# A two-layer attention and convolution kernel: the first part in two passes in written order, and the last part paced with seven image-0 units and a one-image unit at the end

## The chip, the cores and the metric

The kernel runs on one core of one Trainium2 chip. The metric is the device time in microseconds. The times of the kernel before are the median of 3 runs, with the lowest and highest beside it. A profile is one execution of its own; all times within it count from its first instruction. PE is TensorE's matmul, PEld its weight load, DVE VectorE, ACT ScalarE, POOL GpSimd and SP SyncE, which here only issues DMAs.

## The reference

Input x is (2, 256, 64, 64) in fp32: two images of 256 channels and 4096 positions. Two layers follow each other, all in fp32.

```python
# layer 0: attention over all 4096 positions, 8 heads of 32 channels
m = resize(mask, (B, 1, 64, 64), 'bilinear')
q = conv1x1(x, Wq, bq) / sqrt(32); k = conv1x1(x, Wk, bk); v = conv1x1(x, Wv, bv)
fuse = softmax(q k^T) v
x = conv1x1(concat[x, fuse], Wf, bf) * m + x * (1 - m)
# layer 1: channel gate, attention in windows of 8x8, a spatial gate
x = x * sigmoid(relu(x ca_w1 + ca_b1) ca_w2 + ca_b2)
x = x + window_attention(x; qkv_w, out_w)          # 4 heads of 64
x = channel_shuffle(x, groups=4)
y = relu(bn1(conv7x7(x, sa_w1, groups=64)))
y = bn2(conv7x7(y, sa_w2, groups=64))
return x * sigmoid(y)
```

## The kernel before

An image is cut into 8 chunks of 512 positions (CH, NCHUNK). There are three parts.

*First part (L147 to L463).* The small inputs are prepared (mask resized, L147 to L180; batch norms folded into the rows of the 7x7 convolutions, L301 to L400; `w_s`, the DRAM copy of the convolutions' band matrices, filled with zeros at L389). In L204 to L265 each of the 16 chunks of x is loaded and multiplied: q and k (L219) into PSUM pairs of two banks, then v (L244). DVE adds the bias to q and k (L230), ACT squares them with the bias (L231), a matmul with `headsum` adds the squares over a head's 32 channels (L254) and DVE takes their maximum (L265). q, k and v go to DRAM in `q_s`, `k_s` and `v_s` by SP's queue. At the end the largest |q| times the largest |k| decides `flag` (L278), whether exp is safe without subtracting a row maximum; every engine reads it (L1147) and enters arm "a" (safe) or "b". In these inputs it is arm "a". The order of the instructions in this part is left to the framework's scheduler; from the arm on it is the written order (`tc.manual_schedule()`).

*Middle (L1090 to L1118).* One slot is an image, a query chunk, a group of 4 heads and 128 keys: 1024 slots. In each, PE makes the scores of four heads (L580), ACT their exp (L590), PE the products with v (L609), and DVE sums exp in `suma` (L611). Keys and values come in pieces of four slots on SP's queue (L507, L509), two pieces ahead. When a chunk's 64 slots are over, denominators and their reciprocal follow by `at(8..12)` a few slots later, and `stage(b, c)` is queued at 13: a generator that does the rest of the chunk (fuse matmul hy at L677, channel gate, window attention, output projection op at L898, sum into `xo` at L909, which goes to DRAM in `x_s`), one step every fourth slot. `bands()` writes the rows of the convolutions into `w_s` on POOL's queue, one DMA every sixth slot.

*Last part (L1120 on).* The convolutions work in 16 units of 4 channel groups (NU, UG): `conv1` (c1, L987), relu, `conv2` (c2, L1011), tanh (L1021) and scaling (L1027) on ACT, product with x on DVE (L1033), and stores, half on SP and half on POOL (L1039). The generator `convolve()` goes through a list of items (unit, images): units 0 to 8 (EARLY = 9) of image 0, units 0 to 8 of image 1, then units 9 to 15 of both images at once. Items of image 0 can run before the last chunk of image 1 is ready and are put between the steps of its stage:

```python
while later or stages:
    now[0] += 2
    run_later(); run_stages()
    if later or stages:
        next(conv)
staged.append(True)
for _ in conv: pass
```

Each `next(conv)` gives one c1, or one c2, or, from one yield to the next, a gate with its stores and the following c1. Within the generator c1 of item k+1 stands ahead of c2 of item k. Once `staged` is set, items that need image 1 load their x from `x_s` (`xla`). The weights of eight units are held in the buffers of exp (`load_w`, L959); unit u+8 is loaded after the image-1 gate of unit u.

Of the kernel before, what the change touches and what calls it, by code (L numbers as in the profile page):

```python
# [19 lines left out]
P = 128  # L20
KC = C // P
# [10 lines left out]
EARLY = 1 + EB  # L32
# [22 lines left out]
def conv_seq_kernel(ctx: ExitStack, tc: tile.TileContext, a, out):  # L55
# [50 lines left out]
    def load(name, shape, src, eng, pool=const):  # L106
        t = pool.tile(shape, F32, name=name)
        eng.dma_start(t, src)
        return t

# [29 lines left out]

    h2 = H // 2
    mhs = []
    mk = ctx.enter_context(tc.tile_pool(name="mk", bufs=2))
    for b in range(B):

        m3 = mk.tile([h2, 3, h2 + 2], F32, tag="m3", name=f"m3_{b}")
        for n in range(3):
            lo, hi = max(0, n - 1), min(h2, h2 + n - 1)  # L150
            at0 = lo - n + 1
            nc.gpsimd.dma_start(
                m3[at0 : at0 + hi - lo, n, 1 : h2 + 1], a["mask"][b][lo:hi, :]
            )
        nc.gpsimd.dma_start(m3[0:1, 0, 1 : h2 + 1], a["mask"][b][0:1, :])
        nc.gpsimd.dma_start(m3[h2 - 1 : h2, 2, 1 : h2 + 1], a["mask"][b][h2 - 1 : h2, :])
        nc.vector.tensor_copy(m3[:, :, 0:1], m3[:, :, 1:2])
        nc.vector.tensor_copy(m3[:, :, h2 + 1 : h2 + 2], m3[:, :, h2 : h2 + 1])
        mid = mk.tile([h2, h2 + 2], F32, tag="mid", name=f"mid_{b}")
        nc.vector.tensor_scalar_mul(mid, m3[:, 1], 0.75)  # L160
        mv = mk.tile([h2, 2, h2 + 2], F32, tag="mv", name=f"mv_{b}")
        mh = mk.tile([h2, 2, h2, 2], F32, tag="mh", name=f"mh_{b}")
        for o in range(2):
            nc.vector.scalar_tensor_tensor(
                mv[:, o], m3[:, 2 * o], 0.25, mid, ALU.mult, ALU.add
            )
        m75 = mk.tile([h2, 2, h2], F32, tag="m75", name=f"m75_{b}")
        nc.vector.tensor_scalar_mul(m75, mv[:, :, 1 : h2 + 1], 0.75)
        for o in range(2):
            nc.vector.scalar_tensor_tensor(  # L170
                mh[:, :, :, o], mv[:, :, 2 * o : 2 * o + h2], 0.25, m75, ALU.mult, ALU.add
            )
        mhs.append(mh)
    for b, mh in enumerate(mhs):
        for c in range(NCHUNK):
            dst = mask_s[b, c].rearrange("(w r o x) -> o r w x", w=NW, r=4, o=2)
            for o in range(2):
                nc.gpsimd.dma_start(
                    dst[o],
                    mh[4 * c : 4 * c + 4, o].rearrange("p (w x) t -> p w (x t)", w=NW),  # L180
                )


    nm = const.tile([P, B * NCHUNK], F32, name="nm")
    flag = const.tile([1, 1], I32, name="flag")
    with (
        tc.tile_pool(name="w0", bufs=1) as w0,
        tc.tile_pool(name="x0", bufs=3) as x0,
        tc.tile_pool(name="st0", bufs=2) as st0,
    ):  # L190
        def weight(n):
            return load(n, [P, KC, C], a[n].rearrange("(k p) o -> p k o", p=P), nc.scalar, w0)

        wq, wk, wv = weight("WqT"), weight("WkT"), weight("WvT")
        bias = {}
        for n in ("bq", "bk"):
            t = w0.tile([P, KC], F32, name=n)
            for g in range(KC):
                for j in range(HG):
                    h = HG * g + j  # L200
                    nc.scalar.dma_start(
                        t[32 * j : 32 * j + 32, g : g + 1], a[n][h % 2, :, h // 2 : h // 2 + 1]
                    )
            bias[n] = t  # L204

        for b in range(B):
            src = a["x"][b].rearrange("(k p) h w -> p k (h w)", p=P)
            for c in range(NCHUNK):
                x = x0.tile([P, KC, CH], F32, tag="x", name=f"x0_{b}_{c}")
                nc.sync.dma_start(x, src[:, :, c * CH : (c + 1) * CH])  # L210
                sqs = []
                for n, w in (("q", wq), ("k", wk)):
                    s = psum2(f"{n}0_{b}_{c}")
                    for g in range(KC):
                        for kc in range(KC):
                            rhs = x[:, kc, :]
                            if n == "q":
                                rhs = rhs.rearrange("p (r w c) -> p w r c", r=WS, w=NW)
                            nc.tensor.matmul(  # L219
                                s[:, g, :],  # L220
                                w[:, kc, g * P : (g + 1) * P],
                                rhs,
                                start=(kc == 0),
                                stop=(kc == KC - 1),
                            )
                    t = st0.tile([P, KC, CH], F32, tag=n, name=f"{n}st_{b}_{c}")
                    sq = st0.tile([P, KC, CH], F32, tag="sq", name=f"{n}sq_{b}_{c}", bufs=4)
                    bt = bias["b" + n]
                    for g in range(KC):
                        nc.vector.tensor_scalar_add(t[:, g, :], s[:, g, :], bt[:, g : g + 1])  # L230
                        nc.scalar.activation(  # L231
                            sq[:, g, :], s[:, g, :], AF.Square, bias=bt[:, g : g + 1]
                        )
                    sqs += [sq[:, g, :] for g in range(KC)]
                    if n == "q":
                        nc.sync.dma_start(q_s[b, c], t.rearrange("p g n -> p (g n)"))
                    else:
                        for g in range(KC):
                            nc.sync.dma_start(k_s[b, g, c], t[:, g, :])
                s = psum2(f"v0_{b}_{c}")  # L240
                sv = s.rearrange("p a (t o) -> p (a t) o", t=2)
                for m in range(4):
                    for kc in range(KC):
                        nc.tensor.matmul(  # L244
                            sv[:, m, :],
                            x[:, kc, m * P : (m + 1) * P],
                            wv[:, kc, :],
                            start=(kc == 0),
                            stop=(kc == KC - 1),
                        )  # L250

                norms = psum1(f"nrm_{b}_{c}")
                for i, sq in enumerate(sqs):
                    nc.tensor.matmul(  # L254
                        norms[32 * i : 32 * i + 32, :], headsum, sq, start=True, stop=True
                    )
                v = st0.tile([P, KC, 4, P], F32, tag="v", name=f"vst_{b}_{c}")
# [45 lines left out]
    def batch_norm(name, t):  # L303
# [9 lines left out]
        return sc, sh  # L313

    cw = ExitStack()
# [897 lines left out]
```

## Time and profile before

| what | value |
|---|---|
| median of 3 runs | 3078.66 us (3075.16 to 3081.13) |
| the profiled execution: its own time | 3070.01 us |
| its span, first to last instruction | 3068.2 us |
| PE busy | 2988.2 us, 97% |
| DVE busy | 2516.5 us, 82% |
| ACT busy | 2450.6 us, 80% |
| POOL busy | 344.7 us, 11% |
| first scores of the middle start at | 219.07 us |
| last product of the middle ends at | 2821.82 us |
| fuse matmul (hy) of the last chunk starts at | 2846.85 us |
| last PE instruction ends at | 3048.9 us |

The shares are averages over three parts with different limits: a part is to be read from its own timeline. Idle time of an engine counts only where another waits for it. In a timeline each line is a run of like instructions: start, length, engine, line, operation, and in brackets the idle time of the engine before it and what ended it.

### The profile page before, as it was taken

The numbers are of one execution on the slowest core, as the hardware profiler recorded it, in microseconds if no ns is written. First come the engines' busy times: TensorE is split into PE (matmuls) and PEld (weight loads), VectorE is DVE, ScalarE is ACT, GpSimd is POOL, SyncE is SP. The second block draws the span as 40 slices with busy tenths as digits, with TensorE's granted clock in tenths as the row PEclk, the third lists the DMA queues.
The fourth block names the chain that finished last, engine by engine and source line by source line (L and its number), as shares of the span: only waits on it lengthen the run. The fifth ranks groups of instructions, "written<-read, shape, count | busy, mean of one in ns | idle before, by whom it ended". The sixth has DMA issues, their size and how long they took to land.

```text
span 3068.2 us, 61291 instructions
## 1 busy us (share of the span) xinstructions
PE 2988.2 (97%) x25338; PEld 1015.0 (33%) x25338; DVE 2516.5 (82%) x1398; ACT 2450.6 (80%) x4122; POOL 344.7 (11%) x591
## 2 busy tenths in 40 slices
PE   8989989999999999999999999999999999999897
PEld 4442222232222222222232222323232223224675
DVE  3229989999999999998999999999999998988211
ACT  2239879898989898998989898989898988987423
POOL 7110000001010101010101001010101010000346
PEclk9989999999999999999999999999999999999998
DMA  6953112314141413242322214132413242314264
GB/s 197 356 162 76 59 50 64 67 63 72 59 81 60 75 64 69 66 75 68 66 66 61 66 59 73 59 74 61 78 60 68 70 71 66 109 57 134 61 203 97
DMA packets 160352, 264.20 MB, mean 86 GB/s; under 512 B 43944, under 2 KB 62620, under 8 KB 160064
## 3 DMA queue, kind: packets, MB, share of 16 engines
q1 hardware_dynamic: 133664, 221.72, 24.4%
q0 software_dynamic: 22432, 35.91, 8.4%
q8 instruction: 201, 3.29, 0.4%
q10 hardware_dynamic: 3968, 2.57, 0.3%
q14 instruction: 87, 0.71, 0.1%
HBM read 197.89 MB, written 65.21 MB: 86 GB/s over the span
## 4 chain that ended last, share of the span: by engine, by line
PE 70%; DVE 16%; issue 2%; DMA 2%; ACT 2%; POOL 1%; SPq 0%; DVEq 0%; ACTq 0%; POOLq 0%
PE sa L580 28%; PE ava L609 26%; DVE suma L611 15%; PE qka L748 4%; PE hya L677 4%; PE vwa L834 2%; PE c2a L1011 1%; POOL out_dram L1039 1%; PE c1a L987 1%; ACT ea L590 1%; PE opa L898 1%; DMA out_dram<-za 1%; PE sca L782 1%; PE rda L647 1%; PE pta L857 1%
## 5 line engine op out<-in xcount | busy, mean ns | idle before, releaser
L611 DVE TENSOR_TENSOR suma<-suma,ea 128x2048 f32<-128x2048 f32 x960 | 2198.7, 2290 | 86.0 <-ACT ea L590 1.8
L590 ACT ACTIVATE ea<-sa 128x512 f32<-128x512 f32 (+1 forms) x3072 | 2044.2, 745 | 85.0 <-PE sa L580 36.9
L580 PE MATMUL sa<-qa,ka 32*128 32x512 f32 x8192 | 1189.9, 641 | 8.2 <-DMA ka<-ks 8.0
L609 PE MATMUL ava<-ea,va 128*32 128x512 f32 x8192 | 1092.3, 605 | 0.3 <-ACT fa L619 0.3
L580 PEld LDWEIGHTS sa<-qa,ka 32*128 32x128 f32 x8192 | 333.1, 183 | 762.8 <-ACT ea L590 688.6
L609 PEld LDWEIGHTS ava<-ea,va 128*32 128x32 f32 x8192 | 161.6, 108 | 780.6 <-issue 754.3
L924 POOL DMA_DIRECT2D xs<-xo x94 | 65.9, 708 | 2353.5 <-DVE xo L909 2353.4
L1039 POOL DMA_DIRECT2D out_dram<-za x192 | 108.0, 571 | 128.1 <-DVE za L1033 92.4
L748 PE MATMUL qka<-ua,qkv_w 128*128 128x512 f32 x256 | 118.4, 605 | 0.7 <-DVE ua L738 0.7
L1033 DVE TENSOR_TENSOR za<-za,xla 128x768 f32<-128x768 f32 (+1 forms) x16 | 20.9, 1309 | 101.4 <-ACT za L1027 65.0
L1011 PE MATMUL c2a<-yca,wa 32*128 32x192 f32 (+1 forms) x1400 | 100.0, 427 | 0.3 <-ACT za L1021 0.3
L685 ACT ACTIVATE ta<-hya,bf 128x512 f32<-128x512 f32 x32 | 20.2, 684 | 96.9 <-PE hya L677 96.9
L1011 PEld LDWEIGHTS c2a<-yca,wa 32*128 32x128 f32 x1400 | 91.8, 316 | 10.9 <-issue 9.7
L689 DVE TENSOR_TENSOR ta<-ta,mca 128x512 f32<-128x512 f32 x32 | 22.0, 689 | 88.0 <-ACT ta L685 88.0
L1021 ACT ACTIVATE za<-c2a 128x384 f32<-128x384 f32 (+1 forms) x50 | 26.3, 578 | 79.7 <-DMA out_dram<-za 47.9
L803 ACT ACTIVATE ewa<-ewa,mxwa 128x64 f32<-128x64 f32 x256 | 85.5, 362 | 0.0
L611 DVE TENSOR_TENSOR suma<-ea,ea 128x2048 f32<-128x2048 f32 x32 | 73.1, 2286 | 15.0 <-DMA va<-vs 15.0
L231 ACT ACTIVATE qsq<-q,bq 128x512 f32<-128x512 f32 x32 | 22.0, 687 | 74.1 <-DVE qst L230 72.6
L430 POOL DMA_DIRECT2D ws<-r2s x112 | 69.5, 623 | 68.5 <-DMA xs<-xo 33.2
L761 ACT ACTIVATE qka<-qka,qkv_b 128x512 f32<-128x512 f32 x64 | 40.7, 694 | 44.2 <-PE qka L748 44.2
L987 PE MATMUL c1a<-xla,wa 128*32 128x192 f32 (+1 forms) x896 | 58.7, 413 | 14.2 <-DMA xla<-xs 14.2
L230 DVE TENSOR_SCALAR qst<-q,bq 128x512 f32<-128x512 f32 x32 | 24.0, 751 | 59.1 <-PE q L219 41.2
(139 smaller groups left out, 1674.7 us busy)
## 6 DMA issues: line engine op xcount, KB each, us to landing
ka<-ks SPq DMA_DIRECT2D x256, 256.0 KB
va<-vs SPq DMA_DIRECT2D x256, 256.0 KB
ws<-zero POOLq DMA_DIRECT2D x16, 896.0 KB, 17.1
wa<-ws SPq DMA_DIRECT2D x16, 896.0 KB
xs<-xo POOLq DMA_DIRECT2D x78, 140.0 KB, 7.2
xla<-xs SPq DMA_DIRECT2D x23, 420.0 KB
x<-in_x_dram SPq DMA_DIRECT2D x16, 512.0 KB
ks<-kst SPq DMA_DIRECT2D x32, 256.0 KB
```

The source lines that it names most:

```text
L430: nc.gpsimd.dma_start(band2[:, at0 : at0 + step * (n - 1) + 1 : step, :], spread(r2_s[k : k + 1, :, i], n),)
L580: nc.tensor.matmul(heads[j], k[r, cols], q[r, g, :], start=True, stop=not shifted)
L590: nc.scalar.activation(e[:, h, :], tile, AF.Exp, scale=SCALE0)
L609: nc.tensor.matmul(av[r, :], v[:, m % PB, r], e[:, j, :], start=start, stop=stop)
L611: nc.vector.tensor_add(total, first[0] if m == 1 else total, e)
L677: nc.tensor.matmul(s[:, oc, :], wf[:, kc, oc * P : (oc + 1) * P], xw[kc] if kc < KC else f[:, kc - KC, :], start=(kc == 0), stop=(kc == 2 ...
L748: nc.tensor.matmul(s[:, j, :], wqkv[:, kc, o : o + P], u[:, kc, :], start=(kc == 0), stop=(kc == KC - 1),)
L803: nc.scalar.activation(e[:, n, :], e[:, n, :], AF.Exp, bias=mx[:, n : n + 1], accum_out=rs[:, n : n + 1],)
L924: eng.dma_start(x_s[b, n, p + r0 : p + r1].rearrange("r g w -> g r w"), xo[64 * h : 64 * h + 64, oc, r0 - WS * c : r1 - WS * c, :],)
L987: nc.tensor.matmul(s[32 * j : 32 * j + 32, 0 : n * W], w[:, j, d, :], xs[k][:, 0:n, j, d : d + W], start=(d == 0), stop=(d == KS - 1),)
L1011: nc.tensor.matmul(tiles[j // 2][:, j % 2, 0 : n * W], w[r, d], y[r, 0:n, d : d + W], start=(d == 0), stop=(d == KS - 1),)
L1039: eng.dma_start(dst[b, i, r0:r1, UG * u : UG * u + UG, :], z[p + r0 : p + r1, :, nb * m + n, :],)
```

## The change

First part. It now runs under `manual_schedule`, in the order of the text, in two passes. Pass 1 does q and k of all 16 chunks; pass 2 does v. All 16 chunks of x stay in SBUF between them. The squares of a chunk are gathered in one tile, DVE takes the maximum over each four neighbouring positions (a new reduce, 128x2048 to 128x512), and the norm matmuls and their reduce run on a quarter of the columns, one chunk later. The flag is computed while pass 2 runs. The v stores move from SP's queue to POOL's. The preparations become a generator, `prepare`, of which one step follows each chunk, and the loads of the weights of the later parts (`pending`) are issued on ACT, four after a chunk. In the arm a one-element exp (`warm`) is put ahead of the first slot.

Stage. The fuse matmul does the x half for both outputs first, then the half with f.

Last part. EARLY is 7: units 0 to 6 of image 0, units 1 to 6 of image 1, units 7 to 15 of both, and at the end unit 0 of image 1 alone. Ahead of the denominators stand two c1; `later` is stepped by one, with one conv step in it; in the stage a conv step follows only the steps that yield True (hy, u, first and second projection, pt, o). x of the image-1 items is requested at the first resumption after `staged`. Stores alternate between POOL and SP; those of the last item between ACT and SP.

```diff
-EARLY = 1 + EB
+DN = 8
+EARLY = 7
...
+    def prepare(mk, cwp):
...
+        for u in range(NU):
+            nc.gpsimd.dma_start(w_s[u], zero)
+            if u % 4 == 3:
+                yield
...
+        def norms(i, tops):
+            s = psum1(f"nrm_{i}")
+            for n in range(2 * KC):
+                s_ = s[32 * n : 32 * n + 32, 0 : CH // 4]
+                nc.tensor.matmul(s_, headsum, tops[:, n, :], start=True, stop=True)
+            nc.vector.tensor_reduce(nm[:, i : i + 1], s[:, 0 : CH // 4], AX.X, ALU.max)
...
+        for i, (b, c) in enumerate(chunks):
+            load_chunk()
...
+            nc.vector.tensor_reduce(
+                tops, sq.rearrange("p g (n f) -> p g n f", f=4), AX.X, ALU.max
             )
+            if i:
+                norms(i - 1, last)
+            last = tops
+            for t, src in pending[4 * i : 4 * i + 4]:
+                nc.scalar.dma_start(t, src)
+            next(prepared, None)
...
+        for i, (b, c) in enumerate(chunks):
+            s = psum2(f"v0_{b}_{c}")
...
+            for g in range(KC):
+                nc.gpsimd.dma_start(v_s[b, g, c], v[:, g].rearrange("p m d -> p (m d)"))
+            if i == 0:
+                norms(len(chunks) - 1, last)
+                nc.vector.tensor_reduce(top, nm, AX.X, ALU.max)
+            elif i == 1:
...
+                nc.vector.tensor_scalar(flag, prod, (SAFE / SCALE0) ** 2, None, ALU.is_le)
...
-            for oc in range(KC):
-                for kc in range(2 * KC):
...
+            for half in range(2):
+                for oc in range(KC):
+                    for kc in range(KC * half, KC * half + KC):
...
-            yield
+            yield True
...
-        items = [(u, (b,)) for b in range(B) for u in range(EARLY)]
-        items += [(u, tuple(range(B))) for u in range(EARLY, NU)]
+        items = [(u, (0,)) for u in range(EARLY)] + [(u, (1,)) for u in range(1, EARLY)]
+        items += [(u, (0, 1)) for u in range(EARLY, NU)] + [(0, (1,))]
...
+                last = k == len(items) - 1
+                engines = (nc.scalar, nc.sync) if last else (nc.gpsimd, nc.sync)
...
-                            eng = nc.sync if i >= 2 else nc.gpsimd
-                            eng.dma_start(
+                            stores += 1
+                            engines[stores % len(engines)].dma_start(
...
                 conv1(k + 1)
                 yield
+                more()
                 z = conv2(k)
                 yield
+                more()
                 gate(k, z)
...
+        nc.scalar.activation(warm, ones[0:1, 0:1], AF.Exp)
...
-        while later or stages:
-            now[0] += 2
+
+        next(conv)
+        while later:
+            now[0] += 1
             run_later()
-            run_stages()
-            if later or stages:
+            if now[0] == len(slots) + DN:
+                next(conv)
+        while stages:
+            if run_stages():
                 next(conv)
```

The steps of `prepare` between its yields are, in order: loads of mask, bn1 and raw1 (ahead of chunk 0); loads of bj and bn2; loads of raw2, the memsets of m1, m2 and `zero`, and the zero rows of `x_s`; mask arithmetic and its 16 stores, one step per image; the scalings of qkv_b, out_b, ca_b2 and WfT minus the identity; the first add of the three batch norms and their square roots on ACT; the rest of the batch norms; m1, `cbias1` and the store of `r1_s`; m2 in two steps; the store of `r2_s` and the zero writes to `w_s`, four to a step. Their operations are those of the kernel before.

## The prediction

> **What bounds the kernel now.** I read the busy shares by slice, then the busy time by stage, then the timelines of the two ends. The rows by stage (start:end, length, busy time of PE, PEld, DVE, ACT, POOL with counts, clock, DMA share, GB/s):
>
> ```profile
> 0.00:219.00 219.00, 197.60 (x650) 101.77 (x650) 68.79 (x141) 62.98 (x85) 78.66 (x156) 0.97 0.69 242
> 219.00:2822.00 2603.00, 2582.44 (x21557) 749.96 (x21561) 2402.83 (x1215) 2305.93 (x3884) 155.84 (x241) 1.00 0.29 69
> ...
> 2907.00:2920.00 13.00, 0.18 (x4) 0.18 (x8) 1.29 (x2) 1.06 (x2) 1.51 (x3) 0.65 0.45 108
> ```
>
> The middle (2603 us) is PE at 99%, and the change leaves its instructions alone but for an order inside L677. What can move are the first 219 us and the last 246.
>
> First part, TensorE timeline (start, length, instruction, idle before it):
>
> ```profile
> 197.06 3.70 PE L219 MATMUL q<-x,WqT 128*128 128x512 f32 x8
> 200.60 3.60 PE L219 MATMUL k<-x,WkT 128*128 128x512 f32 x8
> 204.03 3.62 PE L244 MATMUL v<-WvT,x 128*128 128x256 f32 x16
> ...
> 208.03 0.60 PE L254 MATMUL nrm<-qsq,headsum 128*32 128x512 f32 x2
> ...
> 219.07 3.79 PE L580 MATMUL sa<-qa,ka 32*128 32x512 f32 x14 [7.96 <-DMA ka<-ks]
> ```
>
> A chunk is 3.54 for q, 3.54 for k, 3.55 for v, about 0.9 for norms: 11.5 us. Sixteen are 184 of the 204 us that the stage takes. Then the flag is made, the branch taken, keys fetched; the first exp starts at 222.47, after a table load of 1.28 us at 221.18. VectorE in a backlogged chunk shows the second limit:
>
> ```profile
> 52.97 0.74 DVE L230 TENSOR_SCALAR qst<-q,bq 128x512 f32<-128x512 f32 x1
> ...
> 54.53 0.75 DVE L230 TENSOR_SCALAR qst<-q,bq 128x512 f32<-128x512 f32 x1
> 55.20 0.74 DVE L230 TENSOR_SCALAR kst<-k,bk 128x512 f32<-128x512 f32 x1
> 56.75 0.75 DVE L230 TENSOR_SCALAR kst<-k,bk 128x512 f32<-128x512 f32 x1 [0.81 <-ACT ksq L231]
> ```
>
> DVE and ACT take turns on one PSUM tile; the last square of this chunk ends at 58.23, 5.26 us after the first start.
>
> Last part:
>
> ```profile
> 2903.05 3.70 PE L898 MATMUL opa<-ota,out_w 128*128 128x512 f32 x8 [1.33 <-ACT ota L887]
> ...
> 2919.82 4.71 PE L987 MATMUL c1a<-xla,wa 128*32 128x192 f32 x56 [13.07 <-DMA xla<-xs]
> 2924.47 3.58 PE L1011 MATMUL c2a<-yca,wa 32*128 32x192 f32 x56
> 2927.98 2.53 PE L987 MATMUL c1a<-xla,wa 128*32 128x192 f32 x56
> ...
> 2985.22 4.80 PE L987 MATMUL c1a<-xla,wa 128*32 128x384 f32 x56
> 2989.95 4.96 PE L1011 MATMUL c2a<-yca,wa 32*128 32x384 f32 x56
> ```
>
> and, in POOL's timeline,
>
> ```profile
> 3048.23 13.45 POOL L1039 DMA_DIRECT2D out_dram<-za x24 [2.87 <-DVE za L1033]
> ```
>
> PE waits 13.07 us for the last chunk to pass through DRAM, its next c1 takes 4.71 instead of 2.53, and after PE ends (3048.9) POOL issues stores for 13 us more. A one-image unit costs 5.97 (2.46 + 3.51), a two-image unit 9.63.
>
> **The Trainium skill.** "PSUM — Partial Sum Buffer", section on bank collisions: ACT and DVE may not read one bank's quadrant at once; the trace agrees with such turns (0.81 and 0.82 us waits). "VectorE: DVE Perf Modes", perf-mode tier table: a reduce has only the one-element rate (0.96 GHz clock there); the trace has 0.69 us for 512 elements (L265, L794), which fits 512/0.96 + 156 ns. "TensorE: Matmul & The Clock Gate", on HAM oscillation: PE drops to half clock after an idle window of about 3.4 us; the c1 of 4.71 agrees. "DMA: Bandwidth & Descriptors", queues and rings: an engine takes its queues in turn; here the burst of zero writes (72 to 126 us, over 400 GB/s) left SP's stores late.
>
> **First part, step by step.**
> *Start.* ACT's bias loads and table load hold its first square to 15.41, as now. In the written order the chain is: q square to 16.1, second q bias and square to 17.64, k to 19.85, then the new reduce to 22.2.
> *New reduce.* 128x2048, by the 512-element row's rate 2048/0.96 + 156 = 2.29 us (a 2048-wide add takes 2.29 too). Not in the trace with groups of four: lower bound 2.2, upper bound twice that; I take 2.29.
> *A chunk of pass 1.* DVE: 5.26 to the last square, 2.25 reduce, 0.22 norm reduce (128 columns): 7.73 us. PE: 7.07 + 0.25 (norms on a quarter of the columns) = 7.3. So DVE with its turns becomes the bound. Fifteen more chunks: 116, to 138.2.
> *Preparation by hand.* Its DVE work now sits in that chain: masks 2.6, scalings 0.9, batch norms 4.0, band rows 2.7 (rows of 17 to 25, 33, 50 to 54 and 63 to 72 us) = 10.2, and about 1.3 for the square-root table load: pass 1 ends at 149.7. Its loads are issued on POOL from 5 us and are down before their chunk; ACT's weight loads, four of about 0.45 us a chunk, lie in the 2.5 us in which DVE reduces. If a load is late, DVE stops and with it the pass.
> *Pass 2.* v of chunk 0 is done before the last norms, which PE awaits until about 150.0; then 15 x 3.55 = 53.2, 0.4 for the flag's row, 1.05 for bvf: 204.7. ACT's copies (1.01 each) fit. The v stores leave SP for POOL, behind 16 zero writes: these become issuable when the band rows are done (about 104) and need 54 us, so v stores land from about 160. Two v buffers and three PSUM pairs hold five chunks, to 164, so PE should not stop. Bounds of the burst: 0 and, as now, 8 us; I take 2. POOL's own issue is 32 x 0.55 = 18 us, against 57 us.
> *Branch.* The flag is ready early, SP can load queries, keys and values during pass 2, and the Exp table load (warm) is behind the last v copy. Each engine reads the flag in 0.49 us and POOL issued 0.6 later, so about 1.1, all of it now on the path: scores at 207.8, first exp at 208.9 against 222.47. That is **-13.6**; if the branch or reused memory holds the loads back to the end of pass 2, 6 us less (the present 212.6 to 219). I book **-13**.
>
> **Middle.** L677 has the same 16 matmuls, x first; ACT waited for the whole pair anyway (2853.96 after 2853.93). Zero; with f ready no less than nothing either.
>
> **Last part.**
> *Before hy.* Last products at 2821.82. Fillers ahead of hy fall from four c1 and three c2 to two and one: 2 x 2.46 + 2 x 3.51 = 11.95 earlier, hy ends at about 2842. f is ready by about 2838 (denominators 3.0 with their gap of 1.07, reciprocal, c2 and its tanh, two copies, one multiply), under the x half of hy.
> *The stage.* Five c1 and five c2 become three and three: 11.9 less. Steps now uncovered: about 0.5 before ca1, 0.5 before ca2 and 2.4 before pt (last exps, v copy, normalise), of which 1.8 to 2.5 was idle before: net -11. The stage's last matmul ends at 2883.8 instead of 2906.7.
> *The wait.* It stays 13.1 us, but c1, c2, c1, c2 of image 0 now stand ahead of the first waiting c1: 11.94. About 1.2 idle, and no slow clock.
> *Units.* 18 single and 7 double become 14 and 9: -4 x 5.97 + 2 x 9.63 = -4.6 us of PE.
> *The end.* The last unit is single and stores on ACT and SP; SP is busy with 12 stores of the double before it until 6.5 us after PE's end, then 6 more at 0.42: 9.0 us of issue after PE against 12.8 now, -3.8.
> Sum: idle -11.9, slow clock -2.2, units -4.6, end -3.8, about 0.5 bubbles: **-22**. Against it: six units in a row fetch weights (917 KB), a double's x and write 256 KB in 5.97 us, 340 GB/s; now three do, and PE lost 1.14 us at 2976. Bounds 0 and 6 more; I take 1: **-21**.
>
> Together -34 on the profiled execution: span 3068.2 to 3034, its own time 3070 to 3036. That execution lies 8.6 under the median; carried to the median 3078.66, **3044.7**.
>
> **Rivals.**
> *Burst and turns eat the first part.* The zero writes meet stores of a faster pass (1.5 MB in 7.73 us is 194 GB/s, in before 2 MB in 11.5) and v stores queue behind them: first part gains 0 to 4, the last part stays: about 3056. For it: DMA share 1.0 from 80 to 130. Against: the x loads end early in the burst, and the stores alone need 129.
> *PE stays the bound.* If DVE and ACT need no turns, or nothing of the burst shows: pass 1 at 7.3, another 6 to 8 us: about 3037.
> *Last part bound by DMA and SP.* The six dense units run at the transfer rate and gates queue behind xla loads: -10 there, 3055.
> *Slower: the reduce with groups of four.* On the path 16 times. At 4.4 us the gain of 34 is used up; at 6.6, three times my value, 16 x 4.3 = +69, net +35: 3114. For it: no such row in the trace. Against: 64-element and whole-row groups cost the same 0.69.
> *The change doesn't do what it says:* the norm bound becomes coarser (it takes the maximum over four tokens), and could send the program into the arm with row maxima. Worked out from the inputs, the product is 16,718 against a limit of 115,200: excluded.
>
> **How the numbers follow.** Forecast 0.58; first part lost 0.13; PE-bound 0.10; last part short 0.08; slower 0.09, and 0.02 where a partly slow reduce cancels the rest. Below 3031 I leave 0.06, above 3067 the 0.11 of the last two: range 3031 to 3067. Within 0.2% (6 us, what this kernel's runs can tell from no change) 0.02; slower 0.09; faster 0.89.
>
> **What would show it.** Right: reduce rows of about 2.3 us, chunks of 7.7 in pass 1, scores near 208 with no wait for ka, under 3 us idle before the first image 1 c1, last POOL store about 8 us after PE. Wrong: a reduce over 4 us; DVE waiting for a load in pass 1; PE idle over 3 us at the v stores or the branch; waits for xla among the units of image 1.

## The result, and the profile after

| | before | after |
|---|---|---|
| median of 5 runs | 3078.79 us (3075.16 to 3081.46) | 3062.25 us (3056.05 to 3067.97) |
| profiled execution: own time, span | 3070.01, 3068.2 | 3056.05, 3054.1 |

The ratio is 0.9955, with a 95% interval of 0.994 to 0.997: faster by 16.5 us in the medians and by 14 in the two profiled executions. The forecast was 3044.7, or 34 us. The direction was right and the time lies in the range, but the forecast gain is twice the measured one.

First the busy time by stage of the kernel after, with the columns of the table shown of before (start:end, length, busy time of PE, PEld, DVE, ACT and POOL, clock, DMA share, GB/s).

```profile
0.00:218.00 218.00, 189.68 (x650) 103.80 (x650) 95.98 (x156) 62.86 (x85) 89.37 (x177) 0.95 0.69 242
218.00:2819.00 2601.00, 2577.62 (x21553) 746.82 (x21557) 2402.40 (x1215) 2305.73 (x3885) 161.92 (x251) 1.00 0.31 69
120.00:130.00 10.00, 9.19 (x28) 3.54 (x27) 4.67 (x5) 2.18 (x4) 2.04 (x4) 1.00 1.02 418
2882.50:2897.00 14.50, 12.82 (x246) 11.74 (x249) 3.12 (x4) 3.84 (x7) 8.23 (x14) 1.00 0.58 123
```

The first part takes 218 us, as long as before. The row 120 to 130 is new: the DMA engines are full at 418 GB/s, and DVE is busy for 4.67 of 10 us. In the last row PE is busy for 12.82 of 14.5 us, where the answering row of before had 0.18 of 13: the wait for the last chunk is covered.

VectorE's timeline of the kernel after, in pass 1 (start, length, instruction, and in brackets the idle time ahead of it with what ended it):

```profile
115.21 2.29 DVE L451 TENSOR_REDUCE top<-sq 128x512 f32<-128x2048 f32 x1 [0.75 <-ACT sq L443]
122.95 2.29 DVE L451 TENSOR_REDUCE top<-sq 128x512 f32<-128x2048 f32 x1 [0.75 <-ACT sq L443]
128.99 0.75 DVE L442 TENSOR_SCALAR qst<-q,bq 128x512 f32<-128x512 f32 x1 [3.56 <-DMA qs<-qst]
...
135.59 0.75 DVE L442 TENSOR_SCALAR kst<-k,bk 128x512 f32<-128x512 f32 x1 [4.28 <-DMA ks<-kst]
...
144.24 0.75 DVE L442 TENSOR_SCALAR qst<-q,bq 128x512 f32<-128x512 f32 x1 [3.16 <-DMA qs<-qst]
...
150.00 0.75 DVE L442 TENSOR_SCALAR kst<-k,bk 128x512 f32<-128x512 f32 x1 [3.44 <-DMA ks<-kst]
...
160.64 2.29 DVE L451 TENSOR_REDUCE top<-sq 128x512 f32<-128x2048 f32 x1 [0.75 <-ACT sq L443]
```

The reduce takes 2.29 us, and between 115 and 123 a chunk takes 7.74. Then DVE stands four times, 14.4 us in all, because the staging tile that it wants to fill is still being stored. In POOL's timeline of the kernel after stand the first and last of the zero writes that were in progress then:

```profile
103.15 4.83 POOL L327 DMA_DIRECT2D ws<-zero  x9
...
129.35 0.53 POOL L327 DMA_DIRECT2D ws<-zero  x1 [2.96 <-DMA ws<-zero]
...
3035.56 6.73 POOL L1096 DMA_DIRECT2D out_dram<-za  x12 [0.63 <-DVE za L1086]
```

The last row is the other end of the kernel: POOL now has 12 stores at the end instead of 24. TensorE's timeline of the kernel after, from the last reduces to the end:

```profile
141.62 6.36 PE L432 MATMUL q<-x,WqT 128*128 128x512 f32 x8
156.03 5.99 PE L469 MATMUL v<-WvT,x 128*128 128x256 f32 x16
...
218.09 3.06 PE L630 MATMUL sa<-qa,ka 32*128 32x512 f32 x16 [1.19 <-ACT vst L477]
237.69 1.14 PE L630 MATMUL sa<-qa,ka 32*128 32x512 f32 x8 [3.36 <-DMA ka<-ks]
...
2832.17 3.70 PE L729 MATMUL hya<-xa,WfT 128*128 128x512 f32 x8
...
2870.14 4.15 PE L1040 MATMUL c1a<-xea,wa 128*32 128x192 f32 x56
...
2896.13 2.54 PE L1040 MATMUL c1a<-xla,wa 128*32 128x192 f32 x56 [1.68 <-DMA xla<-xs]
2898.60 0.78 PE L1064 MATMUL c2a<-yca,wa 32*128 32x192 f32 x4
2902.49 4.87 PE L1064 MATMUL c2a<-yca,wa 32*128 32x192 f32 x52 [3.11 <-ACT za L1074]
2907.29 3.02 PE L1040 MATMUL c1a<-xla,wa 128*32 128x192 f32 x56
```

Behind DVE's waits PE runs slowly (6.36 for a q that took 3.70 in most other chunks). The scores start at 218.09 without a wait for `ka`; one piece later there is such a wait. The c1 of the last chunk waits for 1.68 us instead of 13.07, but its c2 stops after four matmuls for 3.11, and 4.87 and 3.02 show a slow clock.

So the span falls apart as follows (us, both profiled executions; the forecast's column is the prediction's own sum):

| stretch | before | after | change | forecast |
|---|---|---|---|---|
| start to first scores | 219.07 | 218.09 | -1.0 | -11.3 |
| first scores to end of last product | 2603.0 | 2601.1 | -1.9 | -1.7 |
| from there to the start of hy | 24.7 | 13.0 | -11.7 | -11.95 |
| start of hy to the end of the stage's last matmul | 60.0 | 50.3 | -9.7 | -11 |
| from there to PE's end | 142.2 | 152.4 | +10.2 | +5.7 |
| PE's end to the end | 19.3 | 19.2 | -0.1 | -3.8 |
| sum | 3068.2 | 3054.1 | -14.1 | -34 |

The 5.7 is -17.2 for the last part up to PE's end (-22 + 3.8 + 1), less the -22.95 of the two rows above. The ends of the rows are those of the timelines; they differ from the times given at the head (2821.82, 2846.85) by less than 0.3 us. Of the missing 20 us, 10 are lost ahead of the first scores, 4.5 behind the stage, 3.7 at the end and 1.4 in the stage.

What happens in the last row can be read from the last line of the program, where every engine ends. POOL's part of it is an instruction DRAIN (smallest, median and largest duration in ns, then start of the first and of the last in us), of the kernel before and of the kernel after:

```profile
L1213 POOLq DRAIN  x3: 46/112/5284, 3062.1 to 3068.0; - x3
L1281 POOLq DRAIN  x3: 46/112/8971, 3044.3 to 3053.8; - x3
```

In the kernel after SP is through at 3049.5, and the program's end waits for POOL, whose drain started at 3044.3 and takes 8.97 us. In the kernel before it took 5.28.

### The profile page after: what moved, and what is told of

The parts are those of the page before. It is cut to its first block, busy times and chain, and to the rows that moved or that the text cites. A ratio compares the mean times of both kernels' runs of the same rounds, so it can differ in the third digit from the quotient of the medians.

```text
span 3054.1 us, 60829 instructions
## 1 busy us (share of the span) xinstructions
PE 2973.5 (97%) x25114; PEld 1007.6 (33%) x25114; DVE 2543.1 (83%) x1411; ACT 2449.0 (80%) x4115; POOL 358.5 (12%) x617
## 4 chain that ended last, share of the span: by engine, by line
PE 82%; DVE 6%; ACT 2%; DMA 2%; POOL 1%; issue 0%; SPq 0%; DVEq 0%
PE sa L630 34%; PE ava L659 31%; DVE suma L661 5%; PE qka L800 4%; PE hya L729 4%; PE c2a L1064 2%; PE vwa L886 2%; PE opa L950 2%; PE c1a L1040 1%; ACT ea L640 1%; POOL out_dram L1096 1%; PE sca L834 1%; PE rda L697 1%; PE ca2a L772 1%; PE pta L909 1%; PE oa L928 1%
## 5 line engine op out<-in xcount | busy, mean ns | idle before, releaser
L1086 DVE TENSOR_TENSOR za<-za,xla 128x1536 f32<-128x1536 f32 (+1 forms) x16 | 22.5, 1409 | 108.1 <-ACT za L1080 70.8
L443 ACT ACTIVATE sq<-q,bq 128x512 f32<-128x512 f32 x32 | 22.0, 687 | 76.5 <-DVE qst L442 73.2
L432 PE MATMUL q<-x,WqT 128*128 128x512 f32 x128 | 64.1, 647 | 5.7 <-DMA WqT<-in_WqT_dram 5.7
L800 PEld LDWEIGHTS qka<-ua,qkv_w 128*128 128x128 f32 x256 | 46.0, 189 | 71.3 <-issue 58.7
```

The costliest lines, as they stand in the source:

```text
L432: nc.tensor.matmul(s[:, g, :], w[:, kc, g * P : (g + 1) * P], rhs, start=(kc == 0), stop=(kc == KC - 1),)
L800: nc.tensor.matmul(s[:, j, :], wqkv[:, kc, o : o + P], u[:, kc, :], start=(kc == 0), stop=(kc == KC - 1),)
```

## The experiments

My theory after this reading: the halves add up; the first part lost its gain to the burst of zero writes, the last part lost 4.5 us to the order of loads and stores on SP, and the end loses to the number of stores on SP (this last is not what the traces show, see below). The rivals: the first part could gain nothing even without the burst, since DVE sets its pace; the burst may act through SP's order or the number of staging buffers; and the last part may be bound by transfers. Ratios are to the kernel before, run on the same chip beside each, with their 95% intervals. Traces are single executions.

**One half alone.** The first kernel is the kernel before with the new first part and `warm`, the second is the kernel before with the new stage and last part.

```diff
# first half alone, against before
+    def prepare(mk, cwp):
...
+        nc.scalar.activation(warm, ones[0:1, 0:1], AF.Exp)
# last half alone, against before
-EARLY = 1 + EB
+DN = 8
+EARLY = 7
...
+            for half in range(2):
...
+        items += [(u, (0, 1)) for u in range(EARLY, NU)] + [(0, (1,))]
```

> The first part of the change alone, with the last part of the kernel before (warm exp kept). Theory (each half short of its forecast, the two independent): the first scores start near 218 as in the changed kernel, the last product of the middle near 2819, and the last part takes the 246 us of before: about 3 us faster than before, ratio 0.999. Rival (the first part is worth its 13 us and something in the last part takes 10 back): ratio 0.996.

> The first part of before with the changed last part and stage order. Theory: 11 us faster (last product to end 235 us instead of 246), ratio 0.9963. Rival (the two halves depend on each other): clearly less than 8 or more than 14 us.

Measured: the first half alone 3073.49 us, ratio 0.9998 (0.9988 to 1.0007), no difference; the last half alone 3057.02, ratio 0.9946 (0.9932 to 0.996). Together they give 0.9944, and the whole change measured 0.9955 (0.994 to 0.997). So all of the gain is the last part's. Its 15.5 us in the medians lie beyond the 14 that were named as a sign of dependence, but the interval (12 to 21 us) holds 14 as well, and the trace has 234.3 us from the last product to the end instead of 246.1, as expected: a dependence of the halves is not shown. In the first half's trace the scores start at 217.84, 1.2 us before the kernel before, and the middle is 9 us longer (2612.0 against 2603.0). One place of that, in a chunk that took 169.2 us instead of 163.2, is this one, in TensorE's timeline of the first half alone:

```profile
727.29 1.93 PE L658 MATMUL ava<-ea,va 128*32 128x512 f32 x5 [3.37 <-issue]
```

PE stood for 3.37 us in the middle of a group for nothing that the records show, and ran slowly after it. Such stops are in some executions and not in others, at different chunks: three kernels tried below have a chunk of 167.5 to 168.5 us. I found no cause.

A stop of the same kind stands ahead of hy, in TensorE's timeline of the last half alone:

```profile
2834.86 1.25 PE L648 MATMUL rda<-inva,spread_h 32*128 32x128 f32 x16 [2.17 <-issue]
2836.04 6.27 PE L680 MATMUL hya<-xa,WfT 128*128 128x512 f32 x8
```

In the twelve traces with the new last part it takes 0.5 to 3.8 us, and in ten of them the x half of hy is slow, 4.9 to 6.6 us. The kernel after, with 0.51 and 3.70, is the lightest of them. From the last product to hy it takes 13.0 to 17.0 us in these traces, so that the 11.7 of the table is the best case of a gain of 7.7 to 11.7.

**The zero writes spread out.** One write per chunk, on SP behind the k stores, instead of 16 in a row on POOL. The tile of zeros is made at the start for it.

```diff
-        for u in range(NU):
-            nc.gpsimd.dma_start(w_s[u], zero)
-            if u % 4 == 3:
-                yield
...
                 # behind the stores of k of chunk i
+                    nc.sync.dma_start(w_s[i], zeros[0])
```

> The changed kernel, but the 16 zero writes to w_s (14.7 MB) go out on SP's queue, one after the k stores of each chunk, instead of all at once on POOL's queue near 103 us. Theory (the burst of zero writes is what stops pass 1: DVE lost 14.4 us waiting for q and k stores, PE then ran cold): no wait for q or k stores, last reduce of pass 1 near 148 instead of 163, first scores near 203 instead of 218; 14 to 17 us faster than the changed kernel, ratio to before 0.990. Rival (the rate of all transfers is the limit, whenever the zeros are written): the waits spread over the 16 chunks and first scores stay past 213.

**More staging instead.** The zero writes stay, and q and k each get five staging tiles.

```diff
-                t = st0.tile([P, KC, CH], F32, tag=n, name=f"{n}st_{b}_{c}")
+                t = st0.tile([P, KC, CH], F32, tag=n, name=f"{n}st_{b}_{c}", bufs=5)
```

> The changed kernel with five buffers instead of two for the staged q and k, so that their stores may be up to four chunks late; zero writes as in the change. Theory of the burst: DVE's waits for q and k stores fall from 14.4 us to under 3, as the lateness of two chunks fits in the buffers; first scores 205 to 209, unless the v stores, which come after the zeros on POOL's queue, stop pass 2; ratio 0.991 to 0.993. Rival (rate of all transfers): pass 2 stops instead, scores near 216.

Measured: spread out 3047.21 us, ratio 0.9914 (0.99 to 0.9928), better than the change with no overlap of the intervals, if short of the 0.990 expected; more staging 3052.68, ratio 0.9936 (0.9921 to 0.995), which overlaps both and misses what was expected (0.991 to 0.993). The window of the spread kernel that answers to the row 120 to 130 above, and the start of its scores on TensorE:

```profile
120.00:130.00 10.00, 9.73 (x37) 4.01 (x36) 6.86 (x10) 3.41 (x5) 0.00 (x0) 1.00 0.84 300
```

```profile
208.88 3.06 PE L629 MATMUL sa<-qa,ka 32*128 32x512 f32 x16 [1.19 <-ACT vst L476]
```

DVE is busy for 6.86 us of ten instead of 4.67, none of its store waits is left, its last reduce starts at 148.75 instead of 160.64, and the scores start at 208.88 (203 was expected). So the burst took the first part's gain, and what the rival of DVE's pace had said, no gain even then, falls. The writes are the same 16, but both their time and their queue are different; writes spread out on POOL's queue were not tried, so that the two are not told apart. Two early chunks took 9.7 and 9.8 us here: ACT issues its weight loads later, its squares stand behind them, and DVE falls 3.0 us behind the kernel after.

The gain of the runs, 0.41% or 12.6 us, is more than the 9.2 at the scores' start. The rest is at the end. POOL's drain there takes less, from the same view:

```profile
L1280 POOLq DRAIN  x3: 46/112/5447, 3042.0 to 3048.3; - x3
```

It is 5.45 us instead of 8.97, and from PE's end to the end it is 15.7 instead of 19.2. The drain goes with what POOL has issued in the whole kernel: it takes 8.66 to 9.45 us in the six kernels whose v stores and zero writes are both on POOL, and 4.79 to 5.45 in the eight that have only one of the two there, the kernel before among them. The kernel with the first half alone has the last part of before, and its drain takes 9.45 instead of 5.28. So the first half's new order, with the v stores on POOL, made the drain at the other end of the kernel some 4 us longer; moving the v stores alone back was not tried.

In the kernel with more staging DVE's store waits are gone too, but the scores start at 211.81, for this reason (TensorE's timeline):

```profile
141.20 6.57 PE L432 MATMUL q<-x,WqT 128*128 128x512 f32 x8 [7.73 <-DMA x<-in_x_dram]
```

The last load of x, issued on SP at 115.40 during the burst, had not landed: the wait moved from the stores to the load, at about half its size (7.73 instead of 14.4). Here the buffers moved the burst's cost; they did not take it away.

**Squares from the copy in SBUF.** The other limit of pass 1 is that DVE and ACT take turns on a PSUM tile. ACT now squares what DVE has written to SBUF with the bias, so that it leaves PSUM alone. Tried with the burst left in, and together with the spread writes.

```diff
                         nc.scalar.activation(
-                        sq[:, g + KC * (n == "k"), :], s[:, g, :], AF.Square, bias=bt[:, g : g + 1]
+                        sq[:, g + KC * (n == "k"), :], t[:, g, :], AF.Square
```

> The changed kernel with squares taken from the copy in SBUF, and the burst of zero writes left as it is. Theory (turns and burst are two losses that add): pass 1 runs at 7.4 us a chunk until the burst, which starts near 90, takes 14 to 20; first scores at 200 to 206, ratio 0.989 to 0.991. Rival (the turns only hide the burst, and transfers set the end of pass 1): first scores at 212 to 218, ratio 0.993 to 0.995.

> The paced zero writes, and ACT squares the biased q and k out of SBUF, where DVE has put them, instead of reading the PSUM tile in turn with DVE. Theory (the turns on one PSUM tile, 5.26 us to the last square, set the pace of pass 1): DVE's four adds run back to back, a chunk on DVE is 2.75 + 0.7 + 2.25 + 0.2 = 5.9 us plus preparation, PE's 7.3 becomes the bound, pass 1 ends near 140 instead of 151 and the first scores start near 197 to 200; ratio 0.987 to 0.989. Rival (DVE's own work is the bound and the turns are filled otherwise): first scores stay at 207 to 209.

Measured: alone 3044.77 us, ratio 0.9914 (0.9901 to 0.9928); with the writes spread 3025.88, ratio 0.9845 (0.9832 to 0.9858). VectorE's timeline of the kernel with both:

```profile
117.29 1.40 DVE L440 TENSOR_SCALAR qst<-q,bq 128x512 f32<-128x512 f32 x2
120.21 1.41 DVE L440 TENSOR_SCALAR kst<-k,bk 128x512 f32<-128x512 f32 x2 [1.51 <-PE k L430]
122.31 2.29 DVE L450 TENSOR_REDUCE top<-sq 128x512 f32<-128x2048 f32 x1 [0.69 <-ACT sq L441]
124.71 1.40 DVE L440 TENSOR_SCALAR qst<-q,bq 128x512 f32<-128x512 f32 x2
```

Two bias additions now follow each other in 1.40 us, and DVE waits for PE (1.51), so PE is the bound, at 7.42 a chunk. Pass 1 ends its last reduce at 132.02, and the scores start at 187.18, 21.7 earlier than with the writes spread alone. That is twice what I had expected of it, since I had counted the shorter turns and not that the preparations' DVE work, some 10 us in the chain before, then runs in DVE's slack (PE starts a q every 7.42 us through it). In the kernel with the burst left, the scores start at 202.26, as expected, and DVE's store waits show why (its timeline):

```profile
113.48 1.41 DVE L442 TENSOR_SCALAR qst<-q,bq 128x512 f32<-128x512 f32 x2 [3.75 <-DMA qs<-qst]
119.91 1.41 DVE L442 TENSOR_SCALAR kst<-k,bk 128x512 f32<-128x512 f32 x2 [5.02 <-DMA ks<-kst]
...
134.37 1.41 DVE L442 TENSOR_SCALAR kst<-k,bk 128x512 f32<-128x512 f32 x2 [4.41 <-DMA ks<-kst]
```

Five such waits, 19.7 us in all instead of 14.4: the faster pass meets the same burst with more stores per time. The two edits bring 15.8 and 9.2 us to the scores' start one by one, and 30.9 together.

**Three orders of the later parts.** (a) The x load for the first stage leaves SP's order ahead of the first scores for slot 8: SP stood at it, with the keys behind it. (b) The gate with its stores goes ahead of the request of `xla`. (c) The stores of the last three items go over three queues.

```diff
 # (a)
-        load_x(0, 0)
...
+            if i == 2 * PB:
+                load_x(0, 0)
 # (b)
                 z = conv2(k)
                 yield
-                more()
                 gate(k, z)
+                more()
 # (c)
-                last = k == len(items) - 1
-                engines = (nc.scalar, nc.sync) if last else (nc.gpsimd, nc.sync)
+                last = k >= len(items) - 3
+                engines = (nc.gpsimd, nc.sync, nc.scalar) if last else (nc.gpsimd, nc.sync)
```

They were suggested by two places in SP's timeline of the kernel after, and the one in ACT's that answers to the second:

```profile
171.21 0.42 SPq L559 DMA_DIRECT2D va<-vs  x1
221.88 0.38 SPq L570 DMA_DIRECT2D xa<-in_x_dram  x1
...
222.90 2.07 SPq L557 DMA_DIRECT2D ka<-ks  x1
...
2892.53 1.99 SPq L1019 DMA_DIRECT2D xla<-xs  x4
2894.64 24.42 SPq L1096 DMA_DIRECT2D out_dram<-za  x30
```

```profile
2901.95 0.87 ACT L1074 ACTIVATE za<-c2a 128x384 f32<-128x384 f32 x2 [10.51 <-DMA out_dram<-za]
...
3037.66 0.87 ACT L1074 ACTIVATE za<-c2a 128x384 f32<-128x384 f32 x2 [4.18 <-DMA out_dram<-za]
```

SP issued nothing for 50 us until 221.88 (the load waited for the last store out of the v staging tile, whose memory it reuses), and the next keys left only then. Later the output stores stand behind four loads of the last chunk, the tanh two units on waits 10.51 us for its buffer, and PE the 3.11 that were seen above.

> The changed kernel with three edits that act at three places, each read from its own stretch of the trace: x of the first chunk is requested at slot 8 instead of ahead of the first slot; at the first resumption after the last stage, the stores of the gate go out before the loads of x of the image-1 items; the last three items store over POOL, SP and ACT in turn. Theory: (a) no wait of PE for keys near slot 8 (3.4 us in the changed kernel, as SP stood at the x load until the reused memory was free); (b) the wait of the second image-1 c2 for ACT (3.1 us, with a slow clock after it) is gone, since the stores of the unit two before it no longer queue behind loads that wait for the last chunk; (c) from PE's end to the end 14 to 16 us instead of 19.2. Together 9 to 12 us faster than the changed kernel, ratio 0.991 to 0.992. Rival for (a): the keys are late because of the bands' DMAs on POOL, and stay late. Rival for (b): loads come later by the time of the stores, and PE waits 2 to 3 us more for xla instead. Rival for (c): ACT's stores hold back its relu and tanh, and nothing is won.

> The three edits and the paced zero writes together. Theory: the gains lie at separate places and add: paced zeros about 13, the three edits 9 to 12 us under the changed kernel; ratio to before 0.987 to 0.989. Rival (they share a cause): less than 17 us under the changed kernel.

> All of these together: paced zeros, squares from the copy, x at slot 8, gate stores ahead of the loads, last stores over three queues. Theory: first part 20 us and last part 9 us under the changed kernel, ratio to before 0.984 to 0.986. Rival (a faster pass 1 with 2.4 MB a chunk in 7.3 us meets the transfer rate): no better than paced zeros with three edits.

Measured: the three edits 3058.53 us, ratio 0.9953 (0.994 to 0.9967), against 0.9955 without them; with the writes spread 3044.96, 0.9911 (0.9897 to 0.9925), against 0.9914; with the squares as well 3024.31, 0.9845 (0.9831 to 0.9858), against 0.9845. So the three together bring nothing that can be measured: a miss each time. The traces of the first show that (a) and (b) do what they were meant to: no wait for `ka` is left, and behind the first c1 on `xla` there is no wait and no slow clock. TensorE's timeline of the kernel with the three edits:

```profile
2897.22 2.55 PE L1040 MATMUL c1a<-xla,wa 128*32 128x192 f32 x56 [1.54 <-DMA xla<-xs]
...
3028.17 5.24 PE L1064 MATMUL c2a<-yca,wa 32*128 32x192 f32 x56 [2.28 <-ACT yca L1048]
```

The second row is (c) backfiring; ACT's timeline of the same kernel says how:

```profile
3023.43 4.22 ACTq L1096 DMA_DIRECT2D out_dram<-za  x8
3027.70 0.42 ACT L1048 ACTIVATE yca<-c1a,cbias 128x192 f32<-128x192 f32 x1 [6.09 <-DMA out_dram<-za]
...
3033.04 5.39 ACTq L1096 DMA_DIRECT2D out_dram<-za  x8
3038.94 0.87 ACT L1074 ACTIVATE za<-c2a 128x384 f32<-128x384 f32 x2 [7.73 <-DMA out_dram<-za]
```

The relu that PE waits for stands behind eight stores that ACT issues (4.22 us), and the last tanh behind eight more. Against the kernel with (a) and (b) alone PE ends 3.2 us later behind the stage. POOL's last stores wait for that tanh too, and its drain starts later: from PE's end to the end it is 22.9 us instead of 19.2, and in the kernels with the writes spread 19.3 instead of 15.7.

**(a) and (b) without (c)**, first alone, then with the two edits of the first part, and last with a third buffer for the gate (its rival explanation of the end: the last tanh waits for a buffer).

```diff
-                z = pool.tile([P, 4, B * nb * W], F32, tag="z", name=f"z{arm}{k}", bufs=2)
+                z = pool.tile([P, 4, B * nb * W], F32, tag="z", name=f"z{arm}{k}", bufs=3)
```

> The changed kernel with the first two of the three edits only (x at slot 8; gate stores ahead of the loads of x at the first resumption), the stores at the end as in the change. Theory: 2.1 us from the keys and 6 to 7 from the stores, as the trace of the three together showed, now without the loss at the end: 8 to 9 us faster than the changed kernel, ratio to before 0.9915 to 0.993; from the stage's last matmul to PE's end 145 to 147 us instead of 152.4. Rival (the gain was only shifted to the end): the end takes over 21 us after PE and the ratio stays at 0.995.

> Paced zero writes, squares from the copy, x at slot 8, gate stores ahead of the loads; end as in the change. Theory: the gains add to the 48 us of paced zeros with squares from the copy: another 7 to 9, ratio to before 0.981 to 0.983, first scores near 187. Rival: no more than 3 under paced zeros with squares from the copy.

> The same with three gate buffers z instead of two. Theory (at the end the last tanh waits 4.2 us for the stores of the unit two before it): that wait goes, PE's last c2 is not held, and from PE's end to the end 16 to 17 us instead of 19.2; 2 to 3 us faster than the same kernel with two buffers. Rival (the queues' own store issue sets the end): under 1 us.

Measured: (a) and (b) alone 3052.38 us, ratio 0.9941 (0.9928 to 0.9955); with the first part's edits 3020.12, 0.9834 (0.982 to 0.9847); with the third buffer 3019.52, 0.9833 (0.982 to 0.9847). By the trace of the first, from the stage's last matmul to PE's end it is 146.5 us instead of 152.4, and the wait for `ka` (3.36) is gone, which makes the 8 to 9 that were expected or nearly so. But the ratio's interval overlaps that of the change (0.994 to 0.997), and of the kernel with both edits of the first part (0.9832 to 0.9858) that of the second: by the runs it is some 3 to 4 us, not told apart from nothing, and both ratios miss the ranges expected. In the trace of the first the middle holds 7 us of the stops without a cause that were seen above, which hides as much. TensorE's timeline of the fastest kernel but one (the second of the three):

```profile
190.90 3.06 PE L629 MATMUL sa<-qa,ka 32*128 32x512 f32 x16 [1.19 <-ACT vst L476]
...
2869.91 2.54 PE L1039 MATMUL c1a<-xla,wa 128*32 128x192 f32 x56 [1.57 <-DMA xla<-xs]
2872.38 3.58 PE L1063 MATMUL c2a<-yca,wa 32*128 32x192 f32 x56
```

The c2 behind the first waiting c1 takes 3.58, whole and at full clock. The third buffer takes ACT's wait at the last tanh away (4.26 to 1.02 us), and its stores start at 3005.34 instead of 3008.66, but SP ends its 42 stores 11.2 us after PE in both, and in both it is 15.5 to 15.6 us from PE's end to the end. With the shorter drain SP is through within 0.4 us of POOL there, so that SP's issue of stores counts again at the end, and the buffer is worth under 1 us. This family of kernels runs 51.6 us under the kernel before in its group (3020.12 against 3071.76), three times the change's own gain.

## Why the prediction was right in direction and wrong in size

Three terms of the prediction's sum failed: the burst, taken at 2 us and measured at 9.2; the dense units with their loads and stores, taken at 1 and measured at 5.5; and the end, where POOL's drain, 3.7 us longer, was not counted at all. A slow clock in the stage is the 1.4 that is left.

*Step durations: right.* The new reduce took 2.29 us, as priced; the Trainium skill's "VectorE: DVE Perf Modes" (perf-mode tier table: a reduce has the one-element rate only) held for groups of four. A chunk took 7.6 to 7.7 in the quiet stretches, and without the burst the last reduce ends at 151.04, against 149.7 in the prediction. The rival of the slow reduce, the only one on the other side, falls, and the program stayed in arm "a".

*The scores without the burst: right with some luck.* They start at 208.88 in the spread kernel, against 207.8. But the terms written down, 204.7 for the end of the v pass and 1.1 for the branch, add up to 205.8. The v pass ended at 207.69 there, mostly because the v product behind the wait for the last norms took 6.17 instead of 3.72, a slow clock that the prediction left out.

*The burst: the term that failed.* "Bounds of the burst: 0 and, as now, 8 us; I take 2." It measured 9.2 at the scores' start by the spread kernel. The upper bound was carried over from a kernel whose chunk took 11.5 us and hid part of a 54-us transfer; the new chunk of 7.7 us still has two staging tiles for q and two for k, and stores through the same DMA engines. I had looked for the burst's victims among the v stores, behind it on POOL's queue, and it hit the q and k stores on SP's. VectorE's timeline of the kernel before shows that it had done so there too, which the prediction did not price:

```profile
115.87 0.75 DVE L230 TENSOR_SCALAR qst<-q,bq 128x512 f32<-128x512 f32 x1 [5.88 <-DMA qs<-qst]
...
122.27 0.75 DVE L230 TENSOR_SCALAR kst<-k,bk 128x512 f32<-128x512 f32 x1 [4.08 <-DMA ks<-kst]
```

The Trainium skill, "DMA: Bandwidth & Descriptors", section "Issuing engines are not separate DMA queues", says that transfers issued by different engines run on the same 16 DMA engines and interleave; the trace agrees (share 1.02 at 120 to 130, and 14.4 us of store waits on DVE). The prediction had noted that the burst left SP's stores late, and drew no cost from it.

*The branch: nearly right.* Scores followed the v pass by 1.19 us, as worked, but the alternative that I had named, reused memory that holds loads back, came true for x, with the keys behind it on SP: 3.36 us at 237.69. I had looked at the first load of each queue and not at what stands behind a load that waits.

*Ahead of hy: right in this trace.* 11.7 against 11.95, and hy runs its x half while f is finished. The other kernels with the same code gain less here, as told above: the stop of PE and the slow x half were not foreseen, and this execution had little of them.

*The stage: 1.4 short.* The uncovered steps cost what was said (pt 1.95), but the c1 after that wait ran at 4.15 instead of 2.53.

*The wait for the last chunk: right, and then given back.* Idle fell from 13.07 to 1.68. The prediction then says "no slow clock". The slow clock came all the same, from a wait that the change creates: output stores behind four loads on SP, ACT's tanh behind the stores, PE behind the tanh. The kernel with the gate ahead of the loads has neither, and 5.9 us less to PE's end: the forecast's +5.7 for this stretch was +4.3 there. "Bounds 0 and 6 more; I take 1" was the term for it, and "gates queue behind xla loads" stood among the rivals, at 0.08.

*The end: wrong, by a path that was not looked at.* -3.8 forecast, -0.1 measured. The prediction follows SP's stores only. Their issue ended 11.1 us after PE rather than 9.0, but SP is through at 3049.5, 14.6 us after PE, which would have given nearly the end that was forecast (15.5). The program ends 4.6 us later, behind POOL's drain of 8.97 us, which the first part's new order, with the v stores on POOL, made longer than 5.28. In the kernels with the writes spread and the change's own order of last stores, where the drain takes 5.45, PE's end to the end is 15.5 to 16.1.

*The cases.* "Burst and turns eat the first part" (0 to 4 us there; measured 2.8 with the middle) and "last part bound by DMA and SP" (-10; measured -11.3) both came true in size. By mechanism they did in part: stores met the burst, but the q and k stores; gates queued behind the loads, but the dense units did not run at the transfer rate, since their products take 2.54 and 3.58 us as elsewhere. I had weighed the two as alternatives, each with the other half at its full forecast, and left out the case of both, -10 to -14, which is the result. They act in different parts of the kernel, so their chances should have been multiplied, not listed side by side.

## What to carry to other kernels

When a stage is made faster, ask again what its background transfers cost: a bound taken from the slow stage was too small, and here a large transfer that was not urgent did best in even portions behind the urgent stores. An engine's queue can also cost at the very end of the program: follow every queue to its last instruction, not only the one that issues last. For each queue that a change touches, list what stands behind every waiting instruction, loads behind stores and stores behind loads alike, because here a wait of the issuing queue came back two buffers later at the bound engine. Risks in separate stages are combined, not ranked.

## What the runs showed of the hardware that was not expected

- POOL's drain at the end of the program took 5.28 us in the kernel before, 8.97 in the kernel after and 5.45 with the zero writes on SP: it is long in the kernels in which POOL had issued both the v stores and the zero writes, although the last of the zero writes was issued 2.9 ms before it. What in them sets its length was not tried.
- Nine of the zero writes of about 900 KB were issued within 4.83 us on POOL; the other seven went one by one, 2.9 to 4.1 us apart, with POOL waiting for an earlier one to finish.
- TensorE slowed after idle times of 1.58 us (ahead of hy with more staging, whose x half then took 6.29 instead of 3.70 at a granted clock of 0.56), 1.95 (c1 4.15, clock 0.61) and 3.11 (c2 4.87, clock 0.50), which are shorter than the window of about 3.4 us that the Trainium skill gives ("TensorE: Matmul & The Clock Gate", on HAM oscillation). After 1.68 it did not (2.54), nor after 1.89 ahead of hy in the kernel with all edits (3.70, clock 1.00), and with (a) and (b) alone hy was slow after 0.52 (5.40, clock 0.68), so that no length of idle time alone decides it.
- DVE and ACT took turns of 0.75 to 0.82 us over a PSUM pair although DVE's second addition and ACT's first square read its two different banks. So the bank rule that the prediction cites does not by itself account for them. Whether the wait is the tile's or the bank's was not tried; the reader that takes the other's SBUF copy does away with it.
- PE stops without a releaser in the records, in some executions: 3.37 us in the middle of the first half alone, 2.3 and 3.1 with (a) and (b), 4.0 with the three edits and the writes spread; and 0.5 to 3.8 at one place ahead of hy.
